# A two-layer spectral attention kernel: GpSimd's operations wait for DVE operations two back, and scalings and products on disjoint channel groups lose their mutual waits

## The chip, the cores and the metric

The kernel runs on one core of one Trainium2 chip. A core has five engines, each with its own instruction stream: TensorE (PE in the profile), VectorE (DVE), ScalarE (ACT), GpSimd (POOL) and SyncE (SP). In this kernel SP only issues DMA transfers. The engines are ordered against each other by semaphores alone. The metric is the device time of one execution in microseconds (us).

## The reference, cut to what matters

The input is `x` with shape (2, 56, 128, 128): two batches of 56 rows, where the reference's group norm takes the axes as batch, height, width and channel, and the layer itself takes them as batch, 56 tokens and a plane of 128 x 128. Two equal layers follow each other:

```python
x = x + _L0_conv_ref(_gn(x), ...)
x = x + _L1_conv_ref(_gn(x), ...)
```

A layer normalizes each plane, and makes keys, queries and values for 8 heads with spectral convolutions: an FFT over the plane, a product with complex weights for the lowest 16 x 16 modes (and the 16 negative ones), the inverse FFT, plus a scaled copy of the input. Attention goes over the 56 tokens, each with its plane as features. Then come a projection, a residual with instance norm, and two more spectral layers with instance norms, a GELU between them and another residual:

```python
scores = jnp.einsum('baks,bals->bakl', qh, kh) * scale
attn = jax.nn.softmax(scores, axis=-1)
out = jnp.einsum('bakl,bals->baks', attn, vh)
...
att = inorm(out + xa, gan, ban)
an = inorm(att, g2, b2)
h = fno_layer(an, M0w, M0b, M0sw, M0sb, norm=True, act=True)
h = fno_layer(h, M1w, M1b, M1sw, M1sb, norm=True, act=False)
y = inorm(h, gmo, bmo) + att
```

All arithmetic is in float32.

## The kernel before, in words

The kernel keeps both batches' planes in on-chip memory (the tile `X2`, named X in the profile) and works in the space of modes: only 32 x 16 complex modes of each plane matter, and the attention's inner products are taken over modes and corrected by a Gram matrix. Per layer L and batch b the stages are:

- `turned` (L514): PE transposes the plane, ScalarE copies it to the tile P and sums it and its squares.
- `modes` (L607): the mean and the inverse root of the variance (`gs`, `gv`, `sh`) come from the sums, the power on GpSimd (`over_root`). Then, for four groups j of 14 channels, the plane P is scaled in place (`scaled`, on DVE, GpSimd or ScalarE), four products on PE take the group over one axis, and DVE transposes the result into `turns`. More products give the modes `xf`.
- `gram`, `scale_x` (L653: 16 scalings of X by a row `gvr` for a batch, each on DVE or GpSimd), `scores`, `softmax`, `values`, `mixes`, `heads`.
- `norms` (L826): sums, a short chain of operations on 56 x 1 and 56 x 3 columns, two of them powers on GpSimd (the tile `k`), then `rows_of` (L573), three DVE scalings of the unit matrix into the tile `dg`, and a PE product that spreads `dg` over the partitions (`spread`).
- `gelu`: PE builds the hidden planes, ScalarE applies the GELU, PE transposes and goes back to modes.
- `spectrum` (L932): again sums, a chain of some twenty DVE operations on 56 x 1 columns (`c`, `f`, `r`) with two powers on GpSimd, `dg`, `spread`, and the inverse transform.
- `end` (L981): PE builds the output planes, DVE combines them (the P<-P,hs,banks operations), and each half is added to a row block of the raw input that was loaded into a slot of the tiles WU, WT and xr (or, at the very end, X). The adds are on DVE or GpSimd. SP loads and stores the blocks.

Beside that, `prepare` and `build` (L495) make the weights' tiles WU and WT from the raw weights for each layer, and `derive` makes small columns (`der`).

The order of the work is not that of the code. Calls are recorded as units in a `_Book`: an operation on DVE, ScalarE, GpSimd or SP is a unit of its own, and PE's products to the same bank are one unit. `_Book.play` then issues the units in the order of a long literal, `_ORDER`, with an engine for each from `_ENGINES` and a memory bank from `_BANKS`. Some numbers in `_ORDER` stand for idle products on PE (`idle`, L1070). Under `tc.manual_schedule()` each engine executes its operations in the sequence in which `play` issues them, and the framework sets semaphore waits for true dependencies between accesses to the same memory. It compares the memory that two accesses span. The groups of 14 channels in `modes` lie interleaved in the same tile (for every position 56 channels), so that a product on one group and a scaling of another could count as overlapping. Apart from such dependencies an engine goes ahead as far as it can: nothing ties GpSimd's place in its own sequence to DVE's in its own.

Since all recorded operations are issued at one line of `play`, the profile puts nearly all of them at L222; the tiles' names tell them apart.

Of the kernel before, what the change touches and what calls it, by code (L numbers as in the profile page):

```python
# [15 lines left out]
B, K, N = 2, 56, 128  # L16
HEADS = 8
EPS = 1e-5


_KY = np.r_[0:16, -16:0]
# [142 lines left out]
class _Unit:  # L164

    def __init__(self, n, kind):
        self.n, self.kind, self.calls = n, kind, []


class _Book:  # L170

    def __init__(self, engines, banks):
        self.engines, self.banks = engines, banks
        self.units, self.places = [], []
        self.open = self.held = None

    def place(self, banks):
        self.places.append(_Place(len(self.places), banks))
# [6 lines left out]
    def one(self):  # L185
        self.open, self.held = None, True
        yield
        self.open = self.held = None

    def add(self, ways):  # L190
        if "P" in ways:
            out = self.held or ways["P"][1][0].place
            if self.open is not out:
                self.units.append(_Unit(len(self.units), "P"))
                self.open = out
        else:
            self.open = None
            self.units.append(_Unit(len(self.units), "".join(ways)))
        self.units[-1].calls.append(ways)

    def to_ap(self, v, at):
        if not isinstance(v, _View):
# [5 lines left out]
        dims[0][0] = row  # L208
        return bass.AP(whole.tensor, whole.offset + o // 1024 * row + 512 * at[v.place.n] + o % 1024, dims)

    def play(self, order, chosen, at):
        for n in order:
            if n >= len(self.units):
                self.idle(n - len(self.units))
                continue
            u = self.units[n]
            e = chosen.get(n, u.kind[0])
            for ways in u.calls:
                op, args, kw = ways[e]
                args = [self.to_ap(v, at) for v in args]  # L220
                kw = {k: self.to_ap(v, at) for k, v in kw.items()}
                getattr(self.engines[e], op)(*args, **kw)  # L222


class _Engine:
# [8 lines left out]
def _planned(book):  # L234
# [5 lines left out]

_DIGITS = "0123456789abcdefghijklmnopqrstuvwxyzABCDEFGHIJKLMNOPQRSTUVWXYZ"
_ORDER = (
    "00010c0302041R1S7b0x1T1U1W080z1V0C1X1Y0D1Z0f2006212207qYqYqYqYqYqYqY1617130g140y230l240B0h28180e2k4g2g0o251529"
    "0E2a2er2r21o0u090d1p0F1l1m0r2c0b1n260a2b2jqYqYr61i1f272h1q2i2f1gr0r0r0190i0q0p1j1h6w6D1k1c1a1b1d1e0MqWqW394QqZ"
    "qZ1A2d1x3a3b3c5i3d3e3r3s3t3A0j0k3i3j3f3o0w3p3l3m2l1y3k2T0v2m3q1B3g2n452o462q0s0t3n3B2p3u2r1C2s301M1J472t1N1O2u"
    "2V1K1L482Y3h491G1D2Z2X4a0n0m1H2v2x1I2w3x1Q2y1P2U2z2B2A3v404b1r4r4x2C2E2I5P1z1E3w4v1u4e1F2W1s1t5k4c4d5M4f1v2D1w"
    "3y3C3D5l3E3F5m4h4i2S4j3X3z5s5o4p2O3G055N5n5r4k4l4m3H4s2M4n3R7S7Z0P0A3I5p3L3U2P4o3J3S3W3M5t2K2Q3O2N2J2R2G2L5j5g"
    "2F5h5q2H34335u375v3N5G4F3T5H3V5w31355x5y0H4G4H4I8w36384J4K4L326E5z803K828v5f5A5B818x435E5I5K4D445C5D4w5F3P4M55"
    "5W5J3Q0O5L4A5X5O4E5Y3Y5Z0T5Q0J4z58543Z6F4u5T5V6G4q604O4t416162766364785U65660G0I4N104P68696H6I6a4y6J4R4S6b426K"
    "4T6N5c6O4U796e6c0N6d6rco514V6L776f4W6g6j676i6P6h6C8y6M6k5RcD6m4X6l705S6z6n6Bcl6Q6x6p8z4Y6R6S716o6q6T6U6V83726W"  # L250
    "6X6s74736y6Y6u6Z7i7a7j6t6v8A95cxcr7c9ccz4Z967h75844C7k859d868788895d7l9e0S8a8bcC9j9qgv8d4B970K7m7N53cF7n98cH7r"
    "7o7p9r7s9s7q9k9x7u5e7Y5a9l7v7w7f7g9Ecm569m7xcn0L7z997A7B7y9F7C9y9a9G7d9f7e9n7t7F7Dcs9b9zcw7E9g9A8c7G9tcA8e9o9h"
    "9i9L7T577V9S7H7X508B7Icp9u7L529T9U7J9M7K9B9p7U9C9v9N7M7QcE7R9D5b9O9w9H7O9P9I9Q9V9J9R7P9Z9W9Xa68p9Ka0cv9Ya7adaT"
    "a1aeaWaVaU8Cak8E8Da8aXafa2a98Faga359a4cIal8G8H8J8o0Z8mcKaYaZaaarctasb00Rb2b1b3b4a5hRb5ab8I8L8K8N8Mckb6b7b8beb9"
    "bfcybabbbcbdbgamatauanaccG8tahaybhbiaoaFaGbjbkcublbnai8O93bmbo7Waj6Abpbqbr8icqbsbtcJazaAavbwap0QaHaMawaIjxbz12"
    "0UaBaqbAaNaObxbyaJ8U8Z8S94axaCaK8XaD8jkTaPbucSbvcT8YaEcUd3cYaQd4aL8saR8uaSdydz8q8nd5d790bBbDbCdA92bE8rdJdTe4e5"
    "d6dUcjcNbF8hcMbGcVcWdVdKgYbHcPdddobIbJcOdZbKbLfSiQdWdp8ld8dEbMdteecLcZdBbNbObQbScBbPbWefegcReqdLbRbTbXbUbYbV8f"
    "8VbZerdGdeesc0c1cXdfdvdOc2ehetc3c4dac5c6r3c7eidPcQc8c9caewd9cbdqeudw8Pdjdghhevejexr3chdYeyeke9cicfdMendQeldHem"
    "cccdceeodkdhepe6e8cgr7ezeC0YeDeEeAeLdDii8ke7d0eFeBeMdndrfh91gagbgcgdgegffifoeReIeY8geSgpdse0edfjggfpf4dueZfb8T"
    "ebf5eafqeTfcfleG8WeHe1fddNgjgqghgkdlfrgmdm8Rf6gn0WgrdC8QfPfukcf0fkh6fvgoh7h8giglfwf8didFdRf7fMfGeOf1dXh9hagweN"  # L260
    "fQfRfHd1fedxfNfOfIfJfDfxhbhcfWfKg4fUfXfVhdgxfLgyfygzeUhfgsfaiNfzfYhehgileKg9iOgug1gteVg0ftfTinhihjhkhlfZioimg2"
    "fEgAfAgBhmikipgCg8e3isfFg6g3itiqfBihhnfCgDgEg5fghoiugFgGgHiHgIhpd2gJirgPgMivgSiFiIdbiwixgQgTgKhxgNhG0XhHhIiGhJ"
    "iyjEg7iziAiB0ViCe2gLiDiJiEijgVdIiKgRiPhKiXhLf9gOhMiRiLiWhDigeciMhEhzeXgXeJgUiYiZdchqj0hshyj1hNjFj2j6gZoFh0j7j3"
    "gWj4j5jJhOiUj9hPjak9jbhQh4hSkajKhTjHiVhUjPjIh2jch3h5jLhVjDjfhWjOjdjMk3jsj8eQjQjejgjhjkjjjGjijlhXohhYh1oCjNjmjn"
    "jojqjRhZjpf2jSiSk7k4oqf3jTjUiToyjyk1k5jVjWorjXk8jYjZk2jrjtokjvk0hujzkbi1k6dSkjjukkozjwkljAl0kdl1kgkmolfmhvffhr"
    "l2kiePhti9ibiafni6l3l7fskhknoHhCkoksl4hAjCl5kekfkphBlellkql8krktkvoxidkwkOl9owlmkuhwlalni8kxlflbiekylglskzlzi0"
    "jBlhkBkAkCi7l6likDltkFlAlBlcljkGldlklukElolwhFlplvkHkIkJkKkLkMkNlClqkUiclxlGlHlDlrkPlIlJi3i2kWlNkVlOkYlPookQkR"
    "lylEofkSonlKlQlRlFotlLlUlMlSkZlTmQmRmPmO11lVlWomoDm1mmlXmtmnoBm2m3ifmSlYmoeWmTmUmpmulZm8mVmWi4m4mvm5mXm9mYoEmZ"
    "m0i5m6man0n1n2n3n5n4n9m7n6mbmfnamcn7mAn8nbncmHogoumgosmdmimhndnenfngmInhnjnimjnkmJnlmBmCnmmemkoAovmlmwmqnnnomr"
    "nsmxntmDmEmsmykXoGnumFmKmznpoemGmLnvnqmMnroimNoXojp4nznxnwoYoInyoZoRoJnAoKnBopr7nCp1p0oSpaoOphoLnDnFnGnEnHp5nI"  # L270
    "nJoUp7pKpinKnLnNp6nOnMnRnSpLnPnTnQnUpbnVpNpnnWponXpcnYo0nZo1pJpPpMpepur1o2pjo3o4o5pGpCo6pkpDpFpApEp2p3pBoToNr1"
    "r9oao9ppocoMoboPodpqpdo7pvoQqXqXqJqKpIprpTqQpXo8pHp8q6pSqLq7q3qdqRpYq8pQqjq2pWpwpOq4pxpZpUq1q0pRqkqeq5qwqxqMqN"
    "qSqfqaqlqypmqqqDq9qTqmqzqrqgqEqAqsoVp9oWpgpfplpVpspyptqPqOqbqUqcqtqVqhqnqGpzqoqpqFqiqBquqHqvqCqI"
)
_ENGINES = (
    "GADDDDSDDVDDVDDSDDDDDGDDGDDVDDGDDGGGVVGVGGGGVVGVVVVGGVGGGVGGGGGGGPSSPSSPSSPSSPSSPSSPSSPSSPSSPSSPSSPSSPSSPSSPSS"
# [24 lines left out]
def fno_layers(ctx: ExitStack, tc: tile.TileContext, x, out, weights, small, const):  # L301
# [305 lines left out]
    def modes(L, b, stats, st):  # L607
        gs, gv, sh = (sbuf(f"{n}{b}", N, k) for n, k in (("gs", 2), ("gv", 1), ("sh", 1)))
        p = bank()
        mm(p[:, :16], C["group"], stats, True, True)  # L610
        V.tensor_reduce(gs, p[:, :16].rearrange("p (r n) -> p r n", r=2), AX.X, ALU.add)
        tt("V", gv, gs[:, 0:1], gs[:, 0:1], ALU.mult)
        stt(gv, gs[:, 1:2], EPS, gv, ALU.add, ALU.subtract)
        over_root(gv, gv)
        stt(sh, gs[:, 0:1], -1.0, gv, ALU.mult, ALU.mult)
        mid = turns
        midv = grid(mid, 32)
        turned_rows = plane[b].rearrange("p (h q) k -> p q h k", q=4)
        wide = P[b][:, 7168 : 7168 + N]
        for j in range(4):  # L620
            i = 14 * j
            v = plane[b][:, :, i : i + 14]
            scaled("VSG", v, v, gv, sh)
            p = bank()
            for q in range(4):
                mm(
                    p[32 * q : 32 * q + 32, :448].rearrange("p (h i) -> p h i", h=32), C["fw"],
                    turned_rows[:, q, :, i : i + 14], True, True, tile_position=(0, 32 * q),
                )
# [446 lines left out]

    book.idle = idle
    with tc.manual_schedule():
        book.play(*_planned(book))


# [49 lines left out]
```

## Time and profile before

| what | value |
|---|---|
| runs of the kernel | 428.89, 424.11, 427.42 us |
| median | 427.42 us |
| profiled execution, its own time | 421.74 us |
| its span, from the first to the last instruction | 419.6 us |
| mean granted clock of PE | 0.947 |
| PE busy | 369.6 us (88%) |
| DVE busy | 296.0 us (71%), 495 instructions |
| ACT busy | 214.2 us (51%) |
| POOL busy | 198.9 us (47%) |
| DMA | 41.00 MB |

The profiled execution took 2.1 us more than its span, and it is faster than all three timed runs. The profile's timeline shows each operation's start and duration, and in brackets how long its engine had idled before and what ended the wait. Busy shares are means over stages that differ; what a wait is worth is read at its place. "PEclk" is the share of its full clock that PE was granted.

### The profile page before, as it was taken

The page shows a single profiled execution, that of the slowest core. Times are in us where ns is not written, and L with a number is a line of the kernel's source. Part 1 is how long each engine was busy: PE and PEld are TensorE (multiplying, and loading weights), DVE is VectorE, ACT ScalarE, POOL GpSimd, SP SyncE. Part 2 cuts the span into 40 slices and gives each one's busy share as a digit, 9 for nine tenths or more (in the row PEclk, how much of TensorE's full clock was granted, in tenths as well). Part 3 has the DMA queues.
Part 4 walks back from the last instruction along what each step waited for, and adds up shares of the span by engine and source line. Part 5 has one row for each costly group of instructions (what it writes and reads, how often), then busy time and mean ns, then how long its engine had stood idle before and what let it go on. Part 6 is the DMA issues. An engine that isn't in the chain of part 4 may idle for free.

```text
span 419.6 us, 16036 instructions
## 1 busy us (share of the span) xinstructions
PE 369.6 (88%) x7120; PEld 247.3 (59%) x7120; DVE 296.0 (71%) x495; ACT 214.2 (51%) x339; POOL 198.9 (47%) x228
## 2 busy tenths in 40 slices
PE   6776998999897999997898999997899999997940
PEld 3342885897674646644654885985676556554510
DVE  6308669795749574699769758466967775998891
ACT  4774782215385669617456974132549689310000
POOL 5406749543395302095339849114731412065780
PEclk9999999999998899999699999998899999997985
DMA  6889521001302001043463182017640000188656
GB/s 153 184 208 203 107 54 31 3 22 35 88 2 84 29 2 35 6 117 107 139 183 114 45 223 82 3 46 213 208 91 3 2 2 3 55 228 236 200 167 195
DMA packets 28037, 41.00 MB, mean 98 GB/s; under 512 B 10336, under 2 KB 13504, under 8 KB 27968
## 3 DMA queue, kind: packets, MB, share of 16 engines
q1 hardware_dynamic: 27824, 39.80, 35.8%
q8 instruction: 56, 0.92, 0.9%
q10 hardware_dynamic: 144, 0.18, 0.2%
q14 instruction: 13, 0.11, 0.1%
HBM read 24.42 MB, written 14.97 MB: 94 GB/s over the span
## 4 chain that ended last, share of the span: by engine, by line
PE 62%; DVE 12%; DMA 6%; issue 5%; ACT 5%; POOL 3%; SPq 3%; DVEq 0%; POOLq 0%; ACTq 0%
PE banks L222 60%; DVE P L222 5%; ACT P L222 3%; SPq L222 3%; DMA X<-x 3%; DVE f L222 2%; DVE dg L222 2%; PE banks L1072 2%; DMA relay<-xr 2%; ACT banks L222 1%; POOL P L222 1%; DMA sm<-small 1%; POOL X L222 1%; DMA WT<-x 1%; POOL gv L222 0%
## 5 line engine op out<-in xcount | busy, mean ns | idle before, releaser
L222 ACT ACTIVATE P<-banks 128x896 f32<-128x896 f32 (+1 forms) x64 | 61.7, 967 | 31.0 <-PE banks L222 25.9
L222 PE MATMUL banks<-P 128*64 128x56 f32 (+2 forms) x1632 | 63.1, 234 | 0.8 <-issue 0.8
L222 PEld LDWEIGHTS banks<-P 128*64 128x64 f32 (+1 forms) x1632 | 56.7, 143 | 7.4 <-issue 4.3
L222 POOL TENSOR_TENSOR X<-X,gvr 121x512 f32<-121x512 f32 x40 | 52.0, 1318 | 10.0 <-PE banks L222 5.4
L222 PEld LDWEIGHTS banks<-C,P 56*128 56x128 f32 (+3 forms) x1096 | 39.6, 166 | 17.0 <-issue 5.6
L222 PE MATMUL banks<-C,P 56*128 56x56 f32 (+3 forms) x1096 | 47.0, 259 | 2.3 <-DVE P L222 2.2
L222 DVE SCALAR_TENSOR_TENSOR P<-P,hs,banks 128x1024 f32<-128x1024 f32 x32 | 39.6, 1268 | 7.2 <-PE banks L222 7.2
L222 ACT COPY P<-banks 128x896 f32<-128x896 f32 (+4 forms) x35 | 29.7, 871 | 19.4 <-PE banks L222 19.3
L222 PE MATMUL banks<-X,Bs 57*64 57x512 f32 x256 | 34.1, 616 | 0.0
L222 ACT ACTIVATE banks<-P 128x1024 f32<-128x1024 f32 x32 | 32.9, 1029 | 0.7
L1072 PE MATMUL banks<-C 128*128 128x512 f32 (+1 forms) x56 | 29.6, 660 | 4.0 <-DMA C<-const_all 3.5
L222 PE MATMUL banks<-X,BTx 57*64 57x512 f32 x256 | 31.6, 603 | 0.0
L222 PE MATMUL banks<-P,C 128*32 128x56 f32 (+3 forms) x344 | 26.7, 373 | 5.6 <-ACT P L222 4.3
L222 ACT ACTIVATE banks<-banks 128x896 f32<-128x896 f32 x32 | 29.0, 905 | 0.7
L222 PEld LDWEIGHTS banks<-C,X 56*128 56x128 f32 x512 | 19.3, 144 | 11.6 <-issue 7.8
L222 PE MATMUL banks<-C,X 56*128 56x56 f32 x512 | 21.7, 231 | 4.5 <-DMA X<-x 4.5
L222 POOL TENSOR_TENSOR X<-P,WU 128x512 f32<-128x512 f32 x13 | 16.5, 1277 | 18.8 <-DVE P L222 10.7
L222 PE MATMUL banks<-turns,C 128*32 128x224 f32 (+1 forms) x288 | 24.0, 387 | 0.3 <-ACT turns L222 0.3
L222 PEld LDWEIGHTS banks<-P,C 128*32 128x32 f32 (+2 forms) x344 | 12.6, 125 | 17.9 <-ACT P L222 7.2
L222 DVE COPY turns<-banks 128x896 f32<-128x896 f32 x14 | 15.2, 1088 | 10.2 <-PE banks L222 10.1
L222 ACT ACTIVATE P<-P,sh,gv 128x1792 f32<-128x1792 f32 x7 | 13.7, 1980 | 13.5 <-PE banks L222 7.9
L1072 PEld LDWEIGHTS banks<-C 128*128 128x128 f32 x56 | 10.9, 215 | 14.8 <-issue 9.5
(236 smaller groups left out, 701.1 us busy)
## 6 DMA issues: line engine op xcount, KB each, us to landing
X<-x SPq DMA_DIRECT2D x16, 448.0 KB
store<-X SPq DMA_DIRECT2D x32, 224.0 KB
out<-P SPq DMA_DIRECT2D x32, 224.0 KB
WU<-x SPq DMA_DIRECT2D x36, 112.0 KB
X<-store SPq DMA_DIRECT2D x32, 112.0 KB
WU<-store SPq DMA_DIRECT2D x18, 112.0 KB
WT<-x SPq DMA_DIRECT2D x16, 112.0 KB
xr<-x SPq DMA_DIRECT2D x12, 112.0 KB
```

What stands on the lines that cost most here:

```text
L222: getattr(self.engines[e], op)(*args, **kw)
L1072: nc.tensor.matmul(banks[:, n % 8, : N * k].rearrange("p (k m) -> p k m", k=k), lhsT=ident, rhs=_bc(ident, 1, k), start=True, stop=True, s ...
```

## The change

Three things differ.

First, `play` ties GpSimd to DVE. While it issues the units, it keeps the names of DVE's instructions. For each GpSimd instruction it adds a dependency, enforced by a semaphore, on the DVE instruction that stands second to last in the issued order (`LEAD = 2`), unless the GpSimd instruction before had the same one. So a GpSimd operation can start once that DVE operation has ended, while at most the last one before it (and what DVE runs after it) is still open.

Second, in `modes` the scaling and the four products of a group j are recorded inside `book.apart(L, b, j)`. In `play`, instructions of the same (L, b), of different groups and on different engines, are declared to have no dependency on each other. The semaphore waits between them go.

Third, `_ORDER` is another literal. It holds the same numbers. Each engine's own sequence is the same in both programs, instruction by instruction (PE's idle products included), and so are `_ENGINES` and `_BANKS`. What the new literal changes is how the engines' sequences are interleaved when they are issued, and so which DVE instruction is the second to last for each GpSimd instruction.

In the built programs GpSimd's semaphore waits on DVE go from 75 to 171, and its separate wait instructions from 81 to 105; its waits on PE go from 21 to 17.

```diff
+LEAD = 2
...
+    @contextmanager
+    def apart(self, *part):
+        self.part = part
+        yield
+        self.part = None
...
         self.units[-1].calls.append(ways)
+        self.units[-1].part = self.part
...
-    def play(self, order, chosen, at):
+    def play(self, tc, order, chosen, at):
+        parts, vector, last = {}, [], None
...
-                getattr(self.engines[e], op)(*args, **kw)
+                ins = getattr(self.engines[e], op)(*args, **kw).ins
+                if e == "V":
+                    vector.append(ins.name)
+                elif e == "G" and len(vector) >= LEAD and vector[-LEAD] != last:
+                    last = vector[-LEAD]
+                    tc.add_manual_dep(
+                        ins, last, mybir.DependencyInfo(mybir.DependencyClass.Sync, mybir.DependencyReason.SCHED_ONLY),
+                        reason="in step",
+                    )
+                if u.part:
+                    for other, on, part in parts.setdefault(u.part[:-1], []):
+                        if part != u.part[-1] and on != e:
+                            tc.declare_no_dep(ins, other, reason="other columns")
+                    parts[u.part[:-1]].append((ins.name, e, u.part[-1]))
...
 _ORDER = (
...
             v = plane[b][:, :, i : i + 14]
-            scaled("VSG", v, v, gv, sh)
             p = bank()
-            for q in range(4):
-                mm(
+            with book.apart(L, b, j):
+                scaled("VSG", v, v, gv, sh)
+                for q in range(4):
+                    mm(
...
-        book.play(*_planned(book))
+        book.play(tc, *_planned(book))
```

More of the change, by code (lines that the diff above doesn't have):

```diff
@@ L166, in __init__ @@
     def __init__(self, n, kind):
-        self.n, self.kind, self.calls = n, kind, []
+        self.n, self.kind, self.calls, self.part = n, kind, [], None
 class _Book:
@@ L174, in __init__ @@
         self.units, self.places = [], []
-        self.open = self.held = None
+        self.open = self.held = self.part = None
     def place(self, banks):
@@ L248 @@
[L248 to L257, printed above, removed]
@@ new lines @@
+    "053X5M2M1w7Z4d4p2P4f2K5l3C2Q5m2N3D3E5N2J3F4h2R4i5s3G2G4j4k5n2L2F4l5o2H0P4m8w3H4s803I5r8v3U3R4n5p3W7S0A4o3L5t3J"
+    "5g5q3S3O3M345j5h5u3331375G5v3N354F3T4G0H5H4H823V4I5w5x81365y4J384K324w4L6E5z3K435E4E445f5I5A5F5B8x5K0T4D5J5C58"
+    "3P5D554M3Q4q5W0O5L5X4t4A5O0J5Y4z5Q543Y0G105Z3Z4y6F414u5T605V424O6G615c5U6265co667663510I64784N6H4P68696I6a4R4S"
+    "4T6b4U6J4V6K6e6c0N796d6N6r6f4W6g6O77676j6L6i6C6PcD6h8y6k6Mcl5Rcx4X70cr6m5Scz6lcC6QcF6z6n6BcH6x6p8z6o4Y726q6R71"
+    "836S6s6Tcmcn6U8Acs74736Vcw6WcA6X4C6y6Y6t6u6Z7i6v7a7j7c754Z958485869c888789965d9d7h0S8a7k8b9egv8d7l4B979j7m0K7N"
@@ new lines @@
+    "987n539q7r7o5e9r9k7p9s7s9x7Y7q9l7u5a7v7f7w9E9m7g567x9F990L7z7A9y7B9G7y9a7C7d9z9f7t7e8c7F9n7D9g9b7E578e7Gcp9o9A"
+    "9tcE9h507T9L7V9i7H8p9u8Bcv7X9ScI527I8o8m7L9M7JcK9Tct9Bck7U7K9Ucy7M9pcG5b9v8t9C9Ncu7Q8C9O9D8D7R9H9w597O9I9P7P9V"
+    "9Q9J0Z9R9W9Z9K9Xa69YaTa0a7aWada1aVaea8aUakaf8EaX8Fa28G8H8Jaga9aYaaa3aZa4alarb00Rb2b1asamhR8Ib38Kb4ata5b5ab8L8M"
+    "8Nb6au8Oanb7b8acbeahb9bfaobaaybbaibc93bdaFbg8ibhbicqazbjbkcJaG8Ubl8ZbnaAbm8Sajbo947W8XbpaH6A8javbq8Yap8saIbr8u"
+    "aM8qbsbw8naqbt0Qawbz12aNjx0UaBbAaOkTbxaCaJbyaxaDaKaPbucSbvaEaQcTd3cUaLaRd4cYdyaSbBd5dzbDdJcjd790bCdT928rd6cVdA"
```

48 lines of the change are left out of this document (24 added, 24 removed).

## The prediction

> **What bounds the kernel now.** I read the page first, then the waits of TensorE (PE) put down to their releasers, then the timeline around each long one.
>
> ```profile
> span 419.6 us, 16036 instructions
> PE 369.6 (88%) x7120; PEld 247.3 (59%) x7120; DVE 296.0 (71%) x495; ACT 214.2 (51%) x339; POOL 198.9 (47%) x228
> PE banks L222 <- DVE dg L222: 11.7, 4, 3.7
> ```
>
> Columns of the last row: us in total, times, longest. PE works almost without pause, and of its pauses after the start most go to four waits for `dg`, a 56x56 tile that DVE writes. The timeline (start, us, engine, operation, wait before it) shows why the first comes late:
>
> ```profile
> 129.47 2.49 POOL L222 TENSOR_TENSOR X<-X,gvr 121x512 f32<-121x512 f32 x2
> 129.67 3.98 DVE L222 TENSOR_SCALAR dg<-C,k,sm 56x56 f32<-56x56 f32 x1
> 131.94 0.45 POOL L222 TENSOR_TENSOR xr<-xr 128x128 f32<-128x128 f32 x1
> 132.35 1.25 POOL L222 TENSOR_TENSOR X<-X,gvr 121x512 f32<-121x512 f32 x1
> 134.14 0.65 PE L222 MATMUL banks<-dg,ones 56*128 56x168 f32 x1 [2.95 <-DVE dg L222]
> ```
>
> A 56x56 scaling lasts 3.98 us, and ends at 133.65, as the fourth GpSimd (POOL) operation in a row ends (132.35 + 1.25 = 133.60). DVE is held out until the burst is over. In the program's order those X scalings stand behind the `dg` operations; GpSimd had run ahead. It is the same at the other long waits:
>
> ```profile
> 65.07 4.21 DVE L222 TENSOR_SCALAR P<-P,gv,sh 128x1792 f32<-128x1792 f32 x1 [0.82 <-PE banks L222]
> 65.22 3.11 POOL L222 TENSOR_TENSOR WT<-tc,C 128x512 f32<-128x512 f32 x3
> 70.25 1.09 PE L222 MATMUL banks<-WT,xf 64*64 64x256 f32 x16 [1.55 <-DVE WT L222]
> ...
> 196.61 3.70 POOL L222 TENSOR_TENSOR X<-P,WU 128x512 f32<-128x512 f32 x3
> 197.13 3.20 DVE L222 TENSOR_TENSOR f<-f,r 56x1 f32<-56x1 f32 x1
> 200.94 0.37 PE L222 MATMUL banks<-dg,ones 56*128 56x112 f32 x1 [3.70 <-DVE dg L222]
> ...
> 284.71 3.72 POOL L222 TENSOR_TENSOR X<-X,gvr 121x512 f32<-121x512 f32 x3
> 284.78 3.69 DVE L222 TENSOR_SCALAR dg<-C,k,sm 56x56 f32<-56x56 f32 x1 [0.97 <-POOL k L222]
> 288.98 0.55 PE L222 MATMUL banks<-dg,ones 56*128 56x168 f32 x2 [2.43 <-DVE dg L222]
> ...
> 377.72 2.48 POOL L222 TENSOR_TENSOR P<-P,WT 128x512 f32<-128x512 f32 x2
> 378.24 3.20 DVE L222 TENSOR_TENSOR f<-f,r 56x1 f32<-56x1 f32 x1
> 380.17 1.25 POOL L222 TENSOR_TENSOR P<-P,WU 128x512 f32<-128x512 f32 x1
> 382.23 0.77 PE L222 MATMUL banks<-dg,ones 56*128 56x112 f32 x2 [2.58 <-DVE dg L222]
> ```
>
> Each DVE operation ends within 0.1 us of the end of the GpSimd burst (200.33 and 200.31, 288.47 and 288.43, 381.44 and 381.42; the first 0.95 after it, the length of its own work). After each wait the clock falls. In the windows: stretch, its us, busy us by engine, then PEclk, DMA share, GB/s:
>
> ```profile
> 71.45:74.86 3.41, 3.41 (x70) 3.41 (x70) 3.38 (x6) 0.00 (x0) 3.41 (x5) 0.50 0.02 5
> 132.89:139.72 6.83, 5.58 (x66) 3.89 (x70) 4.98 (x12) 1.34 (x2) 2.35 (x4) 0.50 0.40 122
> 201.16:207.98 6.82, 6.82 (x50) 4.91 (x49) 5.08 (x7) 2.90 (x6) 2.82 (x4) 0.50 0.32 97
> 289.90:293.31 3.41, 3.41 (x18) 1.95 (x20) 1.73 (x5) 0.21 (x1) 0.00 (x0) 0.50 0.81 228
> 300.14:303.56 3.42, 3.42 (x41) 2.88 (x38) 3.42 (x3) 0.71 (x2) 0.90 (x3) 0.50 0.82 238
> 382.06:388.89 6.83, 6.66 (x22) 4.22 (x22) 4.94 (x8) 0.00 (x0) 2.88 (x4) 0.50 0.87 257
> ```
>
> PE is busy 3.41 + 5.58 + 6.82 + 3.41 + 3.42 + 6.66 = 29.3 us at half its clock, which is 14.65 us more than at the full one.
>
> **The change part by part.** No instruction is added or removed but waits, and no engine's own sequence moves, SP's neither; only what GpSimd waits for does, and what the scalings and products of one (layer, batch) wait for.
>
> *The lead.* 80 of GpSimd's 224 operations started here before the DVE operation had ended that they would now wait for, from the WU build at 35.11 (its DVE operation, the first of two scalings from 33.35, ended at 36.09) to the last add at 399.81 (its own, the second add from 398.94, at 402.07):
>
> ```profile
> 33.35 4.61 DVE L222 TENSOR_SCALAR P<-P,gv,sh 128x1792 f32<-128x1792 f32 x2
> 35.11 1.90 POOL L222 TENSOR_TENSOR WU<-tc,C 128x512 f32<-128x512 f32 x1
> ...
> 394.88 6.64 POOL L222 TENSOR_TENSOR P<-P,X 128x512 f32<-128x512 f32 x5 [0.19 <-DVE P L222]
> 398.94 3.13 DVE L222 TENSOR_TENSOR P<-P,X 128x512 f32<-128x512 f32 x2
> ```
>
> Place by place, from the new order:
> - 70.25: the second and third WT builds now wait for later DVE operations. The burst ends at 66.3 and not 68.3, so DVE is 2 us earlier: all 1.55 us go.
> - 134.14: the X scalings wait for the second `dg` and what follows it. Nothing of GpSimd stands beside the first `dg`; PE had work until 131.19, and three short operations from 129.67 end before: 2.95.
> - 200.94: the first of the three adds isn't held; it ends at 197.85. DVE is out at about 198.0 in place of 200.33: 2.3 of 3.70.
> - 288.98: the first X scaling isn't held either (ends 285.95), the other two wait for DVE operations behind `dg`: 288.47 - 286.1 = 2.3 of 2.43.
> - 382.23: the first add ends at 378.96, the next waits for the second `dg`: 2.3 of 2.58.
>
> Together 11.4. A smaller case of the same kind:
>
> ```profile
> 295.03 5.26 POOL L222 TENSOR_TENSOR X<-X,gvr 121x512 f32<-121x512 f32 x4
> 296.57 1.37 DVE L222 TENSOR_TENSOR P<-P,tot 128x224 f32<-128x224 f32 x1
> 297.99 0.68 PE L222 MATMUL banks<-C,P 56*64 56x56 f32 x16 [1.16 <-DVE P L222]
> 299.20 2.11 PE L222 MATMUL banks<-P,C 64*128 64x224 f32 x14 [0.54 <-ACT P L222]
> ```
>
> All four scalings now wait for DVE operations that start at 299.51 or later; 1.16 + 0.54 = 1.7 more. In the tail the second add loses its neighbour: 3.13 us for two adds becomes some 2.1, 1.0 less. Sum of waits: **14.1**.
>
> A rule weighs against this. The Trainium skill, "SBUF — State Buffer", section "SBUF: two separate sides", says that DVE and GpSimd share a port pair which the one that starts first holds for its whole instruction. By that a blocked DVE operation would get in after one GpSimd operation; five blocks of 1.3 us would be worth an estimated 6.5 in place of 11.4. The 3.98 us behind four operations don't agree, and I keep the rows.
>
> *The clock.* Where the wait goes, the slow stretch should. At most 14.65. At least what DVE leaves: a stretch can't be shorter than DVE's busy time in it, if all of that is needed there. That allows 0.03, 1.85, 1.74, 1.68, 0 and 1.89 (stretch less DVE): 7.2. The middle is 10.9; I take off 1.7, half of one 3.41 us stretch, for the 1.4 us that stay of the wait at 200.94, since 1.55 us at 70.25 were enough. **9.2**.
>
> *Independent groups.* ScalarE's scalings waited for products on other columns:
>
> ```profile
> 37.17 1.99 ACT L222 ACTIVATE P<-P,sh,gv 128x1792 f32<-128x1792 f32 x1 [6.11 <-PE banks L222]
> 39.21 2.09 PE L222 MATMUL banks<-P,C 128*32 128x448 f32 x20 [2.11 <-ACT P L222]
> ...
> 225.06 1.99 ACT L222 ACTIVATE P<-P,sh,gv 128x1792 f32<-128x1792 f32 x1 [1.83 <-PE banks L222]
> 227.09 0.96 PE L222 MATMUL banks<-P,C 128*32 128x448 f32 x8 [1.35 <-ACT P L222]
> ```
>
> Both start as soon as ScalarE is free. The second saves 1.35; the first between 0 and 2.11, as the last of its products also waits for a DVE transpose: I take 1.3. **2.65**.
>
> *What it costs.* A held operation starts later: GpSimd's 75 waits on DVE become 171 (counted in the two programs), on an engine that is idle 53% of the span. Each push is the end of the DVE operation now waited for less the old start, or what the held operation ahead passes on. Behind a held operation queue the next ones, among them the small powers (`k`, `r`, `vc`) that DVE's chains wait for; by these pushes each of them still finds GpSimd free 1.4 us or more ahead of its start. Three transfers on SP would find their add late, by less than DVE is earlier at the same place. The longest pushes that a reader follows closely are those of the X scalings from 295.03 on, up to 7.7 us, to an end at 308.0; the reader is
>
> ```profile
> 321.18 1.09 PE L222 MATMUL banks<-X,Bs 57*64 57x512 f32 x8
> ```
>
> 13 us later, so nothing waits for them, and if PE gains all of 8 us before that, 5 are left. What remains is that held operations meet other DVE operations. The nearest rows say 1.25 us each; with 80 of them and DVE not on PE's path most of the time I take three on the path, 3.8, with bounds of 0 and the rival below.
>
> Sum: 14.1 + 9.2 + 2.65 - 3.8 = **22.2 us** off. From the profiled execution, 421.74, that is 399.5; from the median of the runs, 427.42, it is 405.2. The runs (424.11 to 428.89) lie above the profiled one; if slow stretches make them differ, fewer of those bring both together. I say **403**.
>
> **The rivals.**
> - *The clock falls anyway.* The half-clock stretches may come from thin work around the waits rather than from them; then 22.2 - 9.2 = 13.0 goes, 408.7 from the profiled execution and 414.4 from the median, so 412. For: a wait of 2.11 us ends at 39.21, and none of the six stretches lies near it. Against: all six begin during a wait named above or within 1.3 us of its end. The Trainium skill, "TensorE: Matmul & The Clock Gate", section "HAM oscillation — how this bites in real kernels", has the clock fall only after idle gaps of some 3.4 us; by that, four of the five waits are too short to matter. Row 70.25, 1.55 us and then PEclk 0.50, doesn't agree.
> - *Slower: the two engines alternate.* A held GpSimd operation starts when the DVE operation two back ends, just when the next DVE operations are due, and can block one for 1.25 us, also in the softmax and `norms` chains that run free today. Each batch of a layer has three such chains that PE may wait for, twelve in all; two blocks in each are 12 x 2 x 1.25 = 30 us, and with PE waiting in all of them the clock gains nothing: 427.42 - 14.1 - 2.65 + 30 = 441. It decides from (14.1 + 9.2 + 2.65) / 1.25 = 21 blocked operations on PE's path out of 80. Against: a GpSimd operation with a wait leaves the gap in which DVE gets in.
> - *The lead isn't kept or changes nothing:* 427. Against: the 80 late starts.
>
> **How the numbers follow.** Forecast 0.72, clock falls anyway 0.13, alternation 0.10, nothing 0.05. The low end is all waits and the whole clock, 14.1 + 14.65 + 2.65 = 31.4 from 421.74, or 390; with a block or two, 392. The high end takes in the first rival with a few more blocks, 417. That leaves the last two out. Measurements of this kernel tell about 1%: faster 0.85, same 0.05, slower 0.10.
>
> **What would show it.** Right: no `dg` or `f` operation of DVE over 1.5 us but where one GpSimd operation stands before it; PE's waits for `dg` at 3 us or less in sum; at most two half-clock stretches; no gap over 1 us between the products in `modes`. GpSimd as busy as before, with more waits on DVE. Wrong: DVE rows of 1 to 1.5 us where there were 0.4, or PE waiting for X, WT or a store behind GpSimd.

## The result, and the profile after

| | kernel before | changed kernel |
|---|---|---|
| runs beside each other | 428.89, 424.11, 427.42, 418.80 us | 395.41, 394.85, 396.05, 394.41 us |
| median | 425.76 us | 395.13 us |
| profiled execution, its span | 421.74, 419.6 us | 395.41, 393.6 us |
| ratio of the times | | 0.9377, 95% interval 0.9270 to 0.9483 |

The change takes 6% off. The ratios here and below leave out runs more than 1.5% above the fastest of their kernel, so that of the kernel before 424.11 and 418.80 us stand here. Beside the experiments below the kernel before ran 11 to 23 more times in each group, with medians of 421.3 to 423.2 us, so some 3 us of the distance between the two medians in the table come from the few runs of the kernel before.

The head of the changed kernel's page, and from its table of waits the row that was 11.7 us in the kernel before:

```profile
span 393.6 us, 16057 instructions
PE 360.3 (92%) x7120; PEld 240.6 (61%) x7120; DVE 279.3 (71%) x495; ACT 213.6 (54%) x339; POOL 200.8 (51%) x228
```

```profile
PE banks L231 <- DVE dg L231: 0.9, 2, 0.8
```

The span is 26.0 us shorter. PE is busy 9.3 us less (369.6 before), with the same products, and it stands idle 33.3 us in place of 50.0, which is 16.7 less. DVE is busy 16.7 us less with the same 495 instructions; 14.0 of that are the five operations that stood blocked (18.3 us in sum before, 4.3 after).

The timeline of the changed kernel at the places that the prediction went through (start, us, engine, operation, wait before it):

```profile
62.41 2.33 DVE L231 TENSOR_SCALAR P<-P,gv,sh 128x1792 f32<-128x1792 f32 x2
67.22 3.12 POOL L231 TENSOR_TENSOR WT<-tc,C 128x512 f32<-128x512 f32 x3
...
125.06 0.29 DVE L231 TENSOR_SCALAR dg<-C,k,sm 56x56 f32<-56x56 f32 x1
125.65 2.51 POOL L231 TENSOR_TENSOR X<-X,gvr 121x512 f32<-121x512 f32 x2 [0.54 <-DVE dg L231]
...
186.04 1.26 POOL L231 TENSOR_TENSOR X<-P,WU 128x512 f32<-128x512 f32 x1
186.56 0.76 DVE L231 TENSOR_TENSOR f<-f,r 56x1 f32<-56x1 f32 x1
187.93 0.36 PE L231 MATMUL banks<-dg,ones 56*128 56x112 f32 x1 [0.79 <-DVE dg L231]
...
270.76 1.26 POOL L231 TENSOR_TENSOR X<-X,gvr 121x512 f32<-121x512 f32 x1
270.83 1.24 DVE L231 TENSOR_SCALAR dg<-C,k,sm 56x56 f32<-56x56 f32 x1 [0.97 <-POOL k L231]
...
357.29 0.76 DVE L231 TENSOR_TENSOR f<-f,r 56x1 f32<-56x1 f32 x1
358.85 0.47 PE L231 MATMUL banks<-dg,ones 56*128 56x112 f32 x2 [0.15 <-DVE dg L231]
361.59 1.78 PE L231 MATMUL banks<-D,C 64*128 64x224 f32 x16 [0.78 <-DVE D L231]
366.14 1.17 PE L231 MATMUL banks<-C,WT 32*128 32x128 f32 x32 [0.65 <-DVE WT L231]
...
373.89 2.06 DVE L231 TENSOR_TENSOR P<-P,X 128x512 f32<-128x512 f32 x2
```

The first `dg` takes 0.29 us where it took 3.98, and the X scalings start behind it. Where the lead lets one GpSimd operation start beside the chain (186.04, 270.76), DVE is held by that one alone: 0.76 and 1.24 us in place of 3.20 and 3.69. The scaling of P at 65 isn't held any more, and the burst of three WT builds comes two microseconds later.

In the windows (stretch, its us, busy us by engine, PEclk, DMA share, GB/s) two stretches at half clock are left within PE's work, of six:

```profile
21.55:24.97 3.42, 3.42 (x32) 2.28 (x29) 0.00 (x0) 1.93 (x5) 0.00 (x0) 0.50 0.93 185
188.81:192.22 3.41, 3.41 (x12) 1.79 (x12) 2.01 (x6) 2.82 (x6) 1.71 (x3) 0.50 0.68 206
```

The second begins 0.9 us after the longer of the two waits for `dg` that are left (0.79 and 0.15 us), as the prediction's reserve of 1.7 us for the clock had it. The first, at 22, has no like in the profiled execution of the kernel before.

### The profile page after: what moved, and what is told of

Its sections match the earlier page's. It is cut to its first block, busy times and chain, and to the rows that moved or that the text cites. A ratio compares the mean times of both kernels' runs of the same rounds, so it can differ in the third digit from the quotient of the medians.

```text
span 393.6 us, 16057 instructions
## 1 busy us (share of the span) xinstructions
PE 360.3 (92%) x7120; PEld 240.6 (61%) x7120; DVE 279.3 (71%) x495; ACT 213.6 (54%) x339; POOL 200.8 (51%) x228
## 4 chain that ended last, share of the span: by engine, by line
PE 64%; DMA 9%; DVE 7%; POOL 5%; issue 4%; ACT 4%; SPq 4%; DVEq 0%; POOLq 0%; ACTq 0%
PE banks L231 63%; SPq L231 4%; DVE P L231 3%; POOL P L231 2%; DMA out<-P 2%; DMA X<-store 2%; ACT banks L231 2%; ACT P L231 2%; POOL X L231 1%; DVE turns L231 1%; DMA X<-x 1%; DMA relay<-xr 1%; DVE X L231 1%; DMA sm<-small 1%; PE banks L1095 1%
## 5 line engine op out<-in xcount | busy, mean ns | idle before, releaser
L231 POOL TENSOR_TENSOR X<-X,gvr 121x512 f32<-121x512 f32 x40 | 53.7, 1349 | 19.7 <-DVE P L231 4.1
L231 PE MATMUL banks<-P 128*64 128x56 f32 (+2 forms) x1632 | 60.1, 228 | 1.1 <-issue 1.1
L231 PEld LDWEIGHTS banks<-P 128*64 128x64 f32 (+1 forms) x1632 | 54.0, 138 | 7.2 <-issue 4.4
L231 PEld LDWEIGHTS banks<-C,P 56*128 56x128 f32 (+3 forms) x1096 | 38.2, 161 | 14.7 <-issue 5.4
L231 PE MATMUL banks<-C,P 56*128 56x56 f32 (+3 forms) x1096 | 45.4, 253 | 0.2
L231 PE MATMUL banks<-P,C 128*32 128x56 f32 (+3 forms) x344 | 25.6, 368 | 2.1 <-DVE P L231 1.3
L231 POOL TENSOR_TENSOR X<-P,WU 128x512 f32<-128x512 f32 x13 | 16.7, 1287 | 16.7 <-DVE P L231 14.3
L231 DVE TENSOR_TENSOR X<-X,gvr 121x512 f32<-121x512 f32 x24 | 22.8, 962 | 0.0
```

The source lines that it names most:

```text
L231: ins = getattr(self.engines[e], op)(*args, **kw).ins
```

## The experiments

Twelve kernels ran, each beside the kernel before. The times, and how long the five DVE operations last that were blocked (the P scaling at 65, then `dg`, `f`, `dg`, `f` in the order of the kernel before):

| kernel | median us | ratio, 95% interval | the five DVE operations, us |
|---|---|---|---|
| before (profiled) | 421.74 | | 4.21, 3.98, 3.20, 3.69, 3.20 |
| changed | 395.13 | 0.938 (0.927 to 0.948) | 1.20, 0.29, 0.76, 1.24, 0.76 |
| apart_only | 416.20 | 0.987 (0.982 to 0.991) | 1.20, 3.99, 3.19, 3.69, 3.20 |
| lead_only | 397.56 | 0.947 (0.942 to 0.952) | 2.17, 0.30, 0.76, 1.25, 0.76 |
| lead_burst | 404.42 | 0.965 (0.959 to 0.971) | 2.17, 0.29, 0.76, 1.24, 0.76 |
| old_order | 420.09 | 0.997 (0.992 to 1.003) | 1.20, 0.29, 0.15, 0.30, 0.14 |
| lead1 | 410.81 | 0.970 (0.963 to 0.977) | 1.20, 0.47, 1.21, 1.24, 1.22 |
| lead4 | 402.56 | 0.951 (0.944 to 0.958) | 1.20, 0.29, 0.76, 1.24, 0.76 |
| fill_before | 422.12 | 0.997 (0.993 to 1.000) | 4.21, 4.00, 3.20, 3.70, 3.21 |
| fill2 | 415.28 | 0.988 (0.985 to 0.992) | 4.20, 4.00, 3.20, 3.70, 3.20 |
| hold3 | 396.22 | 0.944 (0.940 to 0.947) | 1.20, 0.29, 0.14, 0.30, 0.15 |
| fill_after | 395.84 | 0.945 (0.939 to 0.950) | 1.20, 0.29, 0.76, 1.25, 0.76 |

The lengths of the blocked operations come back to 0.02 us from run to run: they follow from the program, not from chance.

### The two edits, one at a time

`apart_only` takes the lead away and keeps the rest:

```diff
-                elif e == "G" and len(vector) >= LEAD and vector[-LEAD] != last:
+                elif e == "G" and False:
```

> The changed kernel without the lead: GpSimd runs as far ahead as before, the declarations and the new interleaving stay (its engines' own sequences are those of the kernel before). My theory: the five bursts of GpSimd block DVE as before; only the waits of 2.11 and 1.35 us go: a ratio of 0.992 to the kernel before, some 3 us. Rival: the declarations matter more, since GpSimd's and ScalarE's scalings start earlier all along: ratio 0.98 or less. The lead's part by my theory is then the rest, some 26 us.

`lead_only` keeps the lead and takes the declarations away:

```diff
-                if u.part:
-                    for other, on, part in parts.setdefault(u.part[:-1], []):
-                        if part != u.part[-1] and on != e:
-                            tc.declare_no_dep(ins, other, reason="other columns")
-                    parts[u.part[:-1]].append((ins.name, e, u.part[-1]))
```

> The changed kernel without the declarations of independence (the lead of two DVE operations and the new interleaving stay). My theory: the two waits of PE for a ScalarE scaling (2.11 and 1.35 us in the kernel before, both gone in the changed one, where 1.0 us came back at the next group) return, so about 2.5 us over the changed kernel's 395.1: 397.6, between 396 and 399. Rival: the lead alone moves the scalings far enough that the declarations do nothing: 395, within 0.5. Rival: a returned wait brings back a stretch at half clock: 400 or more.

The lead is the main part: without it 21 us of the 27 between the medians of 422.2 and 395.1 come back. In `apart_only` the row of PE's waits for `dg` stands as it was:

```profile
PE banks L231 <- DVE dg L231: 11.7, 4, 3.7
```

But the declarations alone gave 1.3%, 5.6 us, in place of the 3 us expected. The rest is at 65 us. In the kernel before, the third P scaling there had first waited 0.82 us for PE's products on another group, and so fell beside the WT builds, which start at 65.22. Without this wait the scalings run through, in `apart_only`:

```profile
62.35 2.32 DVE L231 TENSOR_SCALAR P<-P,gv,sh 128x1792 f32<-128x1792 f32 x2
62.51 3.78 POOL L231 TENSOR_SCALAR P<-sh 128x1 f32<-128x1 f32 x1
67.16 3.11 POOL L231 TENSOR_TENSOR WT<-tc,C 128x512 f32<-128x512 f32 x3
```

This time DVE's operations come back to back and GpSimd is the one that is held: its small operation on P lasts 3.78 us, where it took 1.14 in the kernel before, and the WT builds come two microseconds later. In `lead_only` the wait is there, one WT build slips in, and the lead holds the other two:

```profile
66.11 2.17 DVE L231 TENSOR_SCALAR P<-P,gv,sh 128x1792 f32<-128x1792 f32 x1 [0.81 <-PE banks L231]
66.26 1.06 POOL L231 TENSOR_TENSOR WT<-tc,C 128x512 f32<-128x512 f32 x1
68.66 3.09 POOL L231 TENSOR_TENSOR WT<-tc,C 128x512 f32<-128x512 f32 x2 [1.34 <-DVE P L231]
```

So each edit alone removes PE's 1.55 us, and no slow stretch follows there in either trace. On top of the lead the declarations are worth 2.4 us by the medians (the intervals overlap), near the 2.65 of the prediction. What comes back without them are waits of 0.91 and 0.77 us in `modes`:

```profile
212.64 2.46 PE L231 MATMUL banks<-P,C 128*32 128x448 f32 x24 [0.91 <-ACT P L231]
244.65 2.46 PE L231 MATMUL banks<-P,C 128*32 128x448 f32 x24 [0.77 <-POOL P L231]
```

### The five bursts alone

`lead_burst` is `lead_only` with the lead on 15 of the 224 operations:

```diff
+BURST = (190, 187, 191, 317, 310, 312, 832, 822, 877, 1084, 1085, 1125, 1569, 1570, 1543)
...
-                elif e == "G" and len(vector) >= LEAD and vector[-LEAD] != last:
+                elif e == "G" and n in BURST and vector[-LEAD] != last:
```

> The changed kernel without the declarations, and with the lead on 15 of GpSimd's 224 operations only: those of the five bursts behind which DVE was held in the kernel before (WT builds at 65, X scalings at 129 and 284, adds at 197 and 378). My theory: the gain comes from these places: the waits 12.3 us and most of the lost clock, some 9 us, so a ratio of 0.95 (404 if the kernel before is at 425); what the lead gives elsewhere (1.7 us in the softmax at 297, 1.0 at 110, 1.0 in the tail) is missing. Rival: it is the keeping in step all along that counts, and 15 operations give less than half: ratio 0.97 or more.

The time of 404.4 us is within half a microsecond of the one expected, but that had the kernel before at 425 us and a ratio of 0.95; by the ratio, 0.965, it is 15 us off where `lead_only` takes 22 off. The bursts are two thirds of the lead's gain. The last third lies in places that they don't touch. Of the 6.2 us between the two profiled spans, 3.0 are PE's waits for two softmax chains (1.94 and 1.05 us), which `lead_only` doesn't have. In `lead_burst` GpSimd's free-running X scalings hold a DVE product there:

```profile
79.30 4.28 POOL L232 TENSOR_TENSOR X<-X,gvr 121x512 f32<-121x512 f32 x3 [0.66 <-ACT gvr L232]
82.58 1.25 DVE L232 TENSOR_TENSOR P<-P,tot 128x224 f32<-128x224 f32 x1
83.97 0.68 PE L232 MATMUL banks<-C,P 56*64 56x56 f32 x16 [1.94 <-DVE P L232]
```

### The interleaving

`old_order` is the changed kernel with the literal `_ORDER` of the kernel before, so that the same rule, on the same sequences, waits for other DVE operations.

> The changed kernel with the interleaving of the kernel before: same rule, same sequences of the engines, but 135 GpSimd operations in place of 80 would now wait beyond their old start, by 681 us in sum in place of 228 (worked out from the times of the kernel before), up to 18 us for the X scalings at 285. All five bursts are held here too. My theory: GpSimd's operations have slack for 228 us of pushes but not for three times as much; PE waits for X, WU or adds at some places, and time goes to 400 to 410. Rival: nearly all of GpSimd's work has slack, only the bursts count: within 1.5 us of the changed kernel. Rival: the pushes cost more than the bursts did: slower than the kernel before.

This was the largest surprise. All five operations are free (0.14 to 0.30 us, 1.20 for the P scaling), freer than in the changed kernel, and the whole gain is gone. Now PE waits for what GpSimd writes, 9.1 us in sum, and ten stretches of 3.41 us run at half clock in place of two. Two rows of its waits, which the changed kernel doesn't have, and one place in its timeline:

```profile
PE banks L231 <- POOL X L231: 5.8, 3, 2.5
PE banks L231 <- POOL P L231: 2.3, 3, 0.9
```

```profile
190.76 4.17 POOL L231 TENSOR_TENSOR X<-P,WT 128x512 f32<-128x512 f32 x3
193.75 1.11 PE L231 MATMUL banks<-C,X 56*128 56x56 f32 x16 [2.50 <-POOL X L231]
194.89 0.55 POOL L231 TENSOR_TENSOR f<-f,C 56x1 f32<-56x1 f32 x1
```

Three adds come so late that PE waits 2.50 us for what they write, and behind them on GpSimd stands the power `f`, for which DVE's chain waits 2.99 us. The lead by itself is neither good nor bad; what it does is set by where the order puts each GpSimd operation between DVE's, and the new literal is the part of the change that makes the holds short (228 us of pushes in place of 681, worked out from the times of the kernel before).

### Other leads

`lead1` and `lead4` change one number, `LEAD = 1` and `LEAD = 4`.

> The changed kernel with a lead of one DVE operation in place of two: by the old times 155 GpSimd operations in place of 80 would wait beyond their old start, by 373 us in sum in place of 228. If the cost of holding goes with the sum of the pushes, as the run with the old interleaving has it (453 us more pushes, 25 us more time), this costs 145 x 0.055 = 8 us: 403. If it goes by places (what stands behind a held operation and is waited for), the tight interleaving keeps the cost small: 397. If the two engines alternate and lose at each turn: 410 or more.

> The changed kernel with a lead of four: 39 operations pushed by 140 us in sum by the old times. The first X scaling at 129 and one build at 65 are let go, the rest of the five bursts stays held. My theory: one or two blocks of 1.25 us come back and nothing is won elsewhere: 398, between 396 and 400. Rival (the lead of two still holds too much): below 394.

Both are worse than expected; `lead1` comes out where its expectation had the two engines alternating. In both the rows show a GpSimd operation beside the chain. With a lead of one, the add starts at the end of the DVE operation ahead, which is when `f` starts, and `f` is held for all of it. `lead1`:

```profile
191.46 1.25 POOL L231 TENSOR_TENSOR X<-P,WU 128x512 f32<-128x512 f32 x1
191.52 1.21 DVE L231 TENSOR_TENSOR f<-f,r 56x1 f32<-56x1 f32 x1 [0.66 <-POOL r L231]
193.35 0.36 PE L231 MATMUL banks<-dg,ones 56*128 56x112 f32 x1 [2.40 <-DVE dg L231]
```

With two, the add is half over by then, and `f` loses 0.6 us. With four, the next add comes free between the two `dg` operations and takes the second. `lead4`:

```profile
190.97 1.26 POOL L231 TENSOR_TENSOR X<-P,WU 128x512 f32<-128x512 f32 x1 [0.23 <-DVE r L231]
191.02 1.26 DVE L231 TENSOR_SCALAR dg<-C,c,r 56x56 f32<-56x56 f32 x1
192.33 0.36 PE L231 MATMUL banks<-dg,ones 56*128 56x112 f32 x1 [2.22 <-DVE dg L231]
```

PE's waits for `dg` are 2.9 us with a lead of one, 0.9 with two and 4.6 with four. For `lead4` they explain half of the 7 us to the changed kernel; `lead1` loses its 15.7 over the whole span, at no single place (in the profiled executions it is 5.4 us behind at PE's product at 193, 11.7 at the last `f` and 14.8 at the end). Two is best of the three with this literal; that doesn't say that it would be with another.

### The clock by itself

To part the clock from the waits, `fill_before` and `fill2` put idle products on PE into the waits of the kernel before, into the bank that the waiting product is to write. `fill2` has 1, 3, 4, 2, 1 and 2 of them, `fill_before` 2, 5, 6, 4, 2 and 4:

```diff
+FILL = {352: (2, 1), 476: (3, 3), 751: (6, 4), 1199: (5, 2), 1239: (4, 1), 1490: (4, 2)}
...
         for n in order:
+            if n in FILL:
+                for _ in range(FILL[n][1]):
+                    self.fill(FILL[n][0])
```

> The kernel before with idle products (128x512, some 0.53 us each at full clock) added on PE just ahead of the six products that wait: 2 at 70, 5 at 134, 6 at 201, 4 at 289, 2 at 298, 4 at 382. They end before the wait does, so PE still waits for the same DVE operations, but is busy meanwhile. It parts the clock from the waits. My theory: the clock falls because PE stands idle for most of one 3.41 us stretch, so the slow stretches behind these six places go and the waits stay: 9 to 13 us off, a ratio of 0.975. Rival (the clock falls anyway, for thin work around the waits or by its own law): ratio 1.00, and the same stretches at half clock. Rival (the extra products only push PE's work back): 1.01 or more.

> The run with idle products ahead of the waits, with fewer of them: one such product takes PE two passes, 0.89 us in the trace of that run and not 0.53, so its five took 4.56 us in a wait of 2.95 and its six 5.31 in one of 3.70, and the products behind them came late. Now 1 at 70, 3 at 134, 4 at 201, 2 at 289, 1 at 298, 2 at 382: each sum lies inside its wait. My theory: the slow stretches behind the six places go, the waits stay, 9 to 13 us off: ratio 0.975. Rival: the half clock costs PE less than its rows say, since what PE does in those stretches waits for other engines anyway: ratio 0.99 to 1.00.

The first one missed by its own sizes: its five products at 134 took 4.56 us,

```profile
133.09 4.56 PE L1082 MATMUL banks<-C 128*128 128x512 f32 x10
```

and what the clock gave was paid back in late products. In `fill2` they fit, and none of the six slow stretches is left. It is worth 1.2%, 5.0 us (3.5 to 6.5 by the interval), half of what was expected. The profiled executions say more. In that of `fill2` three other stretches are slow, one at 21 and two around the wait of 2.11 us at 39, which in the profiled execution of the kernel before had cost no clock:

```profile
38.52:41.93 3.41, 2.52 (x16) 0.79 (x20) 2.27 (x3) 3.41 (x7) 0.29 (x1) 0.50 0.94 205
41.93:45.35 3.42, 3.42 (x36) 1.50 (x30) 2.87 (x6) 0.27 (x2) 1.47 (x3) 0.50 0.92 199
```

The first idle product stands at 70, and up to there the two programs are the same, so these stretches aren't the experiment's doing. They put this execution 1.9 us behind (the third P scaling starts at 66.99 in place of 65.07), and at its end it is 7.2 us ahead. In this pair the six places are thus worth some 9 us with the waits kept.

The same shows without any edit. `port` and `port2` (below) are the kernel before, instruction for instruction, up to a section behind its end. Its waits come back in them: 1.55 and 1.54 us at the place of 70.25, 2.96 and 2.96 at 134.14, 3.70 and 3.71 at 200.94, 2.43 and 2.42 at 288.98, 2.58 and 2.58 at 382.23. The slow stretches don't. Before PE's work ends, the profiled execution has nine of 3.41 us, `port` eight and `port2` six, and in `port2` none follows the waits of 1.54, 2.42 and 2.58 us. So a wait of this length can bring a slow stretch, but needn't. In the 61 runs of the kernel before beside the experiments the time goes with the granted clock, from 416.19 us at 0.964 to 428.48 us at 0.923. A line through them, with the time at half clock taken as twice the missing share of the clock, gives an estimate of 1.2 us for each stretch, 11 for nine. So the six places are worth some 5 to 11 us when the waits stay, and the waits themselves are the larger part.

`fill_after` puts five such products into waits of the changed kernel (at 21, 31, 37 and 188).

> The changed kernel with five idle products on PE inside waits that it still has: two (0.89 us each) in the 2.25 us at 21, one in the 1.66 at 31, one in the 1.26 at 37, and a short one (0.45 us) in the 0.79 at 188. My theory: the two slow stretches that the changed kernel shows (3.41 us at 22 and at 189) go, 1.7 us each at most, and by the run with idle products in the kernel before about half of that counts: 393 to 394.5 in place of 395.1, a ratio of 0.935. Rival: nothing in the first 40 us counts, since the loads set the pace there: 395 and the same ratio as the changed kernel, 0.938. Rival: the products push PE's work back: 396 or more.

The time is that of the changed kernel, as the first rival had it, but for another reason. Both slow stretches are gone, and at 233 the execution is 2.0 us ahead of the changed kernel's; most of that goes in a wait of PE of 2.37 us at 235 and a new slow stretch at 237. The span is 393.5 us.

### Holding the last three

`hold3` moves the three GpSimd operations that still start beside a chain to places behind it.

```diff
+    for late, ahead in ((832, 752), (1084, 1113), (1569, 1564)):
+        order.remove(late)
+        order.insert(order.index(ahead) + 1, late)
```

> The changed kernel with three GpSimd operations moved later in the interleaving: the first add at 188 (behind the second dg of spectrum), the first X scaling at 271 and the first add at 357. They are the three that the lead of two lets start beside the chain: in the changed kernel they block one DVE operation each (f 0.76, dg 1.24, f 0.76 us). My theory: f and dg fall to 0.15 and 0.29, PE's waits of 0.79 at 188 and 0.15 at 359 go, and the one slow stretch behind the first (3.41 us at half clock, 1.7 us) goes too: 392.5 to 394.5 in place of 395.1. Rival: what stands behind the held operations on GpSimd comes late by as much: 395 or more.

`f` and `dg` come free, as expected, PE's wait of 0.79 falls to 0.17, and the slow stretch behind it goes; a new one comes at 237. A DVE operation further on pays:

```profile
187.45 2.90 POOL L231 TENSOR_TENSOR X<-P,WU 128x512 f32<-128x512 f32 x2 [1.33 <-PE banks L1098]
189.27 1.13 DVE L231 TENSOR_SCALAR D<-D,C 128x56 f32<-128x56 f32 x1
190.79 1.03 PE L231 MATMUL banks<-D,C 64*128 64x224 f32 x8 [1.40 <-ACT P L231]
```

Two adds now stand back to back, and the scaling of D behind `dg`, 0.25 us in the changed kernel, takes 1.13. PE waits 1.40 us where it didn't wait before. (The row names ScalarE; the operation that PE reads, D, ends at 190.40, and 190.64 with the second one on it.) The time is not below that of the changed kernel. No version beat it.

### The block by itself

`port` and `port2` measure how long GpSimd holds DVE, in a section behind the kernel's end: each trial a small GpSimd copy, five X scalings by ones, and one DVE operation that the copy releases.

```diff
+                g.tensor_copy(col, ones[:, :1])
+                for n in range(5):
+                    ...
+                    g.tensor_tensor(w, w, _bc(ones[: 64 + K + 1, :], 1, 4), ALU.mult)
+                test()
```

> The kernel before with a measuring section behind its end, some 100 us long: 14 trials, in each a small GpSimd copy, then five X scalings of 121x512 (by ones, so that nothing changes) back to back on GpSimd, and beside them one DVE operation that the small copy releases: a 56x56 scaling like dg, a 56x1 product like f, scalings of 128x56, 128x512 and 128x1792, a product of 128x512, and a 128x512 scaling out of PSUM; then the same seven behind a DVE operation out of PSUM, so that they start later in the burst. My theory: DVE operations that read only SBUF are held until the burst of five ends, 5 x 1.26 = 6.3 us; the one out of PSUM isn't held. By the rule that the lock is held for one instruction each gets in after one GpSimd operation, 1.3 us. The trace of before speaks for a third possibility: the small ones (56 partitions) are held for the whole burst, the large ones get in after one.

> The measuring section again, for why the kernel's DVE operations were held through a whole burst and 13 of the 14 in the first section only through one GpSimd operation. There every X scaling of GpSimd also waited on GpSimd's own semaphore, for an older scaling of the same rows. Now six trials on rows of their own, so that the scalings wait for nothing of GpSimd's, and the six again, where the scalings carry no wait at all. If a wait on its own semaphore is what opens the gap, the DVE operations are held for the five, 6.3 us, above all in the second pass. If what DVE does decides, the times are those of the first section: 1.2 us for the small ones, 1.5, 1.7 and 2.1 for the larger.

The theory that a DVE operation is always held to the end of the burst fell in both runs. Of 24 trials on operations that read only SBUF, 22 got in as soon as the GpSimd operation in progress ended, of all sizes, and two, both the 128x56 scaling, were held to the end of the burst (5.45 and 6.11 us). The same scaling got in at once in its two other trials. The two out of PSUM weren't held (0.74 and 0.75 us). `port2`, second pass, where no scaling carries a wait:

```profile
445.89 6.14 POOL L1097 TENSOR_TENSOR X<-X,ones 121x512 f32<-121x512 f32 x5
445.97 1.22 DVE L1084 TENSOR_SCALAR dg<-C,gv 56x56 f32<-56x56 f32 x1 [4.94 <-POOL gv L1093]
...
458.33 6.14 POOL L1097 TENSOR_TENSOR X<-X,ones 121x512 f32<-121x512 f32 x5
458.40 6.11 DVE L1086 TENSOR_SCALAR WM<-WM,gv 128x56 f32<-128x56 f32 x1 [5.03 <-POOL gv L1093]
```

So both things happen: a blocked DVE operation usually gets in after one GpSimd operation, and now and then it waits for the whole burst. A wait on GpSimd's own semaphore isn't what decides, nor is the size alone. In the kernel before, five places are of the second kind, with the same lengths in all five traces of its sequence (its own, `fill_before`, `fill2`, `port`, `port2`); why these is open.

## Why the prediction was right

It came out on its side and inside its range (392 to 417), 8 us below the 403 that it named, of which 4 are its sum and the others its place between two bases.

- **The waits.** 14.1 us were forecast. The five waits fall from 13.2 to 0.9, which is 12.3 (forecast 11.4); the softmax waits at 298 go whole, 1.7; the two tail adds take 2.06 us in place of 3.13, 1.1. That is 15.1. The step that sized the remains was right in kind: at 201 and 382 one add stays beside `f`. It is half over when `f` comes, which the prediction put 0.6 us too dear at 201. (The 0.95 us by which the P scaling at 65 outlasts the burst isn't the length of its own work, as the prediction reads it; free, it takes 1.20.)
- **What it missed.** PE's 1.05 us in the other softmax at 110 went too (0.07 after). The rows in the kernel before, of the kind that the prediction had found at 297, a DVE product beside an X scaling:

```profile
107.09 1.26 POOL L222 TENSOR_TENSOR X<-X,gvr 121x512 f32<-121x512 f32 x1
107.22 1.38 DVE L222 TENSOR_TENSOR P<-P,top 128x224 f32<-128x224 f32 x1
110.23 0.67 PE L222 MATMUL banks<-C,P 56*64 56x56 f32 x16 [1.05 <-DVE P L222]
```

- **Independence.** 2.65 forecast; 2.4 measured on top of the lead. The first wait of 2.11 did leave 0.81 for a DVE transpose, as the step supposed, and 2.11 - 0.81 + 1.35 is 2.65 again. What the step didn't see is that the declarations also free the scaling at 65.
- **The clock.** 9.2 forecast, and PE's busy time fell by 9.3; nine slow stretches have become two, and the reserve of 1.7 us was for one like that at 188.81. The size of the term is less sure than this agreement: with the waits left in place the same stretches are worth 5 to 11 us by the experiments. What the step had wrong is that every slow stretch belongs to its wait. It read one execution, and in `port2` the waits of 1.54, 2.42 and 2.58 us had none behind them.
- **The price.** 3.8 us were set for holds that meet other DVE operations. What looks like it are new waits of PE of 0.78 and 0.65 us at 361.59 and 366.14. But `port2`, where nothing is held, has them too, 0.62 and 0.66 us, where the slow stretch at 382 is missing. So hardly any of the 3.8 us shows, and the term was too dear. That the pushed operations have slack held, with the new literal; `old_order` shows the same rule costing the whole gain. The prediction worked its pushes out from the new order and so had this right, but the way in which the term can eat the gain is not the one it named for its upper bound of 30 (DVE blocked again): it is GpSimd's own work that comes late.

Of the rivals, the clock did not fall anyway: the stretches went with the waits, and with products in the waits. The alternation of the two engines is real, 1.2 us each time in `lead1`; in the changed kernel the three chains lose 0.6, 0.9 and 0.6 us to it. The rule of the Trainium skill, "SBUF — State Buffer", section "SBUF: two separate sides", that the lock is held for the whole of one instruction, read as the prediction read it (DVE gets in after one GpSimd operation), agrees with 22 of 24 trials and not with the five bursts of this kernel. For this kernel's sum the rows were the better base.

## What to carry to other kernels

When a short DVE operation lasts several microseconds, look at what GpSimd runs beside it: here 53% idle on GpSimd's side said nothing, since its work stood in bursts, ahead of time, exactly beside the short chains that PE waits for. Holding GpSimd back by a wait on DVE paid only with an issue order that puts its operations behind the chain and not far behind: with another interleaving the same waits ate the whole 26 us. Change the waits and the order together, and count for each held operation what stands behind it on its engine.

## What the runs showed of the hardware that was not expected

The stretches at half clock lie on a grid. In the kernel before they start at 71.45, 132.89, 201.16, 289.90, 300.14 and 382.06 us; the differences are 18, 20, 26, 3 and 24 times 3.413 us. Ahead of each of them PE was idle for much of the stretch before. The stretches ahead of three of them, and one in the kernel before that was followed by full speed (the first row):

```profile
37.31:40.73 3.42, 1.52 (x16) 0.55 (x20) 3.06 (x4) 3.42 (x4) 1.31 (x1) 1.00 0.92 194
68.03:71.45 3.42, 1.87 (x28) 0.89 (x28) 3.42 (x7) 0.00 (x0) 3.32 (x3) 1.00 0.00 0
129.47:132.89 3.42, 1.72 (x41) 1.23 (x40) 3.37 (x2) 2.75 (x4) 3.42 (x5) 1.00 0.32 91
197.74:201.16 3.42, 0.22 (x5) 0.22 (x6) 3.15 (x4) 2.04 (x6) 2.58 (x3) 1.00 0.74 215
```

PE was busy 0.22 to 1.87 us of 3.42 ahead of these slow stretches, so no gap of the whole stretch is needed: 1.55 us of waiting were enough at 70. The busy time isn't the whole law, as the first row shows; in `port` the same wait of 1.55 us falls in a stretch with PE busy 1.86 us, and full speed follows. The Trainium skill, "TensorE: Matmul & The Clock Gate", section "What's actually happening", has such a window, of 3413 ns and free-running; the grid agrees. Its place isn't tied to the program's start: the stretches that begin at 71.45 us in the kernel before and at 37.76 in `port2`, each counted from its own first instruction, are 9.87 times 3.413 us apart. So the same wait can fall differently on the grid from one execution to the next. That the time of the kernel before varies with its granted clock fits this; no run here shows what moves the grid, or whether it alone decides which stretches are slow.
